# A convolution gate in front of a self-attention: the norm and pooling of the next image pair in pieces inside the attention loop

## The chip, the cores and the metric

The kernel runs on one core of one Trainium2 chip. The metric is the device time of one execution in microseconds (us). Five engines run their own instruction streams in order: PE (TensorE, matrix products), DVE (VectorE), ACT (ScalarE, which holds one set of function tables at a time), POOL (GpSimd) and SP (SyncE, which issues the DMAs here). Matrix products land in PSUM.

## The reference

A tensor `x` of 8 x 64 x 64 x 64 (images, channels C, rows, columns) goes through four layers: layer 0 is a selective scan followed by a gate (`_safm`), layer 1 a channel and a spatial self-attention, layer 2 a network with two inner training steps, layer 3 another spatial self-attention. The change touches the gate of layer 0 and the spatial attention of layer 1:

```
xo = (scan part of layer 0)
return xo + _safm(_channel_ln(xo, cn_g, cn_b), mfr_w, mfr_b, aggr_w, aggr_b)

def _channel_ln(x, g, b):                      # mean and variance over the channels
    return (x - u) * rsqrt(v + 1e-6) * g + b
def _safm(x, ...):                             # channels in 4 parts of 16
    for i in range(4):
        s = parts[i]; k = 2 ** i
        if i > 0: s = max-pool of s, k x k     # 32x32, 16x16, 8x8
        s = 3x3 depthwise convolution of s     # mfr_w[i]
        if i > 0: s = each value repeated k x k
    out = 1x1 convolution of all four parts + aggr_b
    return gelu(out) * x

# layer 1, per image; x is 64 channels x 4096 positions n
x1 = gamma_ca * (channel attention of x) + x
energy_s = q^T k                               # 4096 x 4096, q and k have 16 rows
out_s = v @ softmax(energy_s)^T
return x1 + gamma_sa * out_s + x
```

## The kernel before

`gate_and_attention` takes the images in four pairs; the two images of a pair lie on partitions 0 to 63 and 64 to 127, a row of 4096 positions each. For each pair `p` it does, in the order in which the code is written:

- **Load and norm.** `x` (2 MB, two buffers) is loaded. `Common.pair_norm` centres the channels with a matrix product (`cps`, L137: four tiles of 1024 positions, two products of 512 each), copies the centred values into the padded plane `pads[0]` (DVE, L140), squares them (ACT, L142) and averages the squares with a product that collects all eight blocks of 512 positions in one PSUM tile `var` of 16 rows (L145). Then come epsilon (DVE, L150), one square root (ACT, L151), one reciprocal (DVE, L152), and for each tile a product that spreads the 16 rows over the channels (`rps`, L157), a multiplication into the plane (DVE, L162) and gain and offset (ACT, L163).
- **Pooling.** Three levels of maxima over the whole plane, horizontally into `max1..3` (L1473) and vertically into `pads[1..3]` (L1475), on DVE.
- **Moves.** A convolution with 3 rows of taps is done as one product over 48 partitions per image (16 channels times 3 row offsets) for each of 3 column offsets. `move` (L1423) brings the three row offsets side by side: 6 DMAs from a plane to a tile `moved[i][r]` of 16 rows (32 rows of level 1 are two moves). A pair needs 8 moves, 48 DMAs, all issued by SP: four for level 0 in three rotating tiles, two for level 1, one each for levels 2 and 3.
- **The convolutions** (`conv`, L1433): levels 3, 2 and 1 (the root, whose results are doubled in size and added up by DVE), then four steps `j` of 1024 positions of level 0, each followed by an addition (DVE, L1454), GELU (ACT, L1504) and two POOL instructions (L1505, L1506) that put the result back into `x`.
- **Channel attention** (transposes and products, L1517 to L1543) and the projections `k` and `v` (`Attention.project`).
- **Spatial attention** (`Attention.run`): eight blocks `i` of 512 queries, each in 16 groups `g` of two key tiles `j`: four score products into two PSUM tiles `sc` (L1179; PSUM pool `sc` has three tiles of two banks, shared with `cps`, `rps` and the convolutions), two exponentials (ACT, L1184, into six rotating `ex` buffers), two additions to the running sum (DVE, L1191), and the products with `v` of the group before (L1198). At `g == 1` the next queries are projected, at `g == 3` `divide` sums and inverts (L1209 to L1219, a DVE reciprocal of 512 columns among it), at `g == 6` `finish` adds the channel mix (`fps`, L1548), writes `x2t` (L1550) and stores it. `qps`, `sumps` and `fps` share one PSUM bank of tag `mm`.

The order within each engine is not that of the code line by line: a planner at build time orders instructions by written priority, by when it reckons their inputs ready, and by free buffers, and adds the waits. Instructions that touch one PSUM bank from two engines are put one after the other. Layer 3 uses the same `Attention` class.

Of the kernel before, what the change touches and what calls it, by code (L numbers as in the profile page):

```python
# [10 lines left out]
F32 = mybir.dt.float32  # L11
BF16 = mybir.dt.bfloat16
AF = mybir.ActivationFunctionType
ALU = mybir.AluOpType
# [4 lines left out]
NB = 8  # L19
C = 64  # L20
S = 64
L = S * S
BK = 512
NBK = L // BK
# [20 lines left out]
class Common:  # L45
# [60 lines left out]
    def pair_norm_consts(self):  # L106

        nc = self.nc  # L110
        cen = self.tile([2 * C, 2 * C], "p_cen")
        nc.vector.memset(cen, 0.0)
        avg = self.tile([2 * C, 4 * NBK - 2], "p_avg")
        nc.vector.memset(avg, 0.0)
        for e in range(2):
            rows, m = slice(e * C, (e + 1) * C), 2 * NBK - 2 + e
            nc.vector.tensor_scalar(
                cen[rows, rows], self.ident[rows, rows], -1.0 / C, None, ALU.add
            )
            nc.vector.memset(avg[rows, m : m + 1], 1.0 / C)  # L120
        spread = self.tile([2 * NBK, 2 * NBK, C], "p_spread")
        nc.vector.tensor_copy(
            spread,
            self.ident[: 2 * NBK, : 2 * NBK].unsqueeze(2).to_broadcast([2 * NBK, 2 * NBK, C]),
        )
        return cen, avg, spread

    def pair_norm(self, work, sc, var, src, dst, consts, eps, g, b):

        nc = self.nc
        cen, avg, spread = consts
        for i in range(NBK // 2):
            ps = sc.tile([128, 2, BK], F32, name="cps", tag="sc")
            for e in range(2):
                nc.tensor.matmul(  # L137
                    ps[:, e, :], cen, src[:, bass.ts(2 * i + e, BK)], start=True, stop=True
                )
            nc.vector.tensor_copy(dst(i), ps.rearrange("p e (r c) -> p (e r) c", c=S))  # L140
            sq = work.tile([128, 2, BK], F32, name="sq", tag="blk", bufs=3)
            nc.scalar.activation(sq, ps, AF.Square)  # L142
            for e in range(2):
                m = 2 * (NBK - 1 - 2 * i - e)
                nc.tensor.matmul(  # L145
                    var[: 2 * NBK], avg[:, m : m + 2 * NBK], sq[:, e, :],
                    start=(i + e == 0), stop=(2 * i + e == NBK - 1),
                )
        rstd = work.tile([2 * NBK, BK], F32, name="rstd", tag="rstd", bufs=1)
        nc.vector.tensor_scalar(rstd, var[: 2 * NBK], eps, None, ALU.add)  # L150
        nc.scalar.activation(rstd, rstd, AF.Sqrt)  # L151
        nc.vector.reciprocal(rstd, rstd)  # L152
        for i in range(NBK // 2):
            ps = sc.tile([128, 2, BK], F32, name="rps", tag="sc")
            for e in range(2):
                j = 2 * (2 * i + e)
                nc.tensor.matmul(  # L157
                    ps[:, e, :], spread[:, j : j + 2, :].rearrange("k e c -> k (e c)"), rstd,
                    start=True, stop=True,
                )  # L160
            out = dst(i)
            nc.vector.tensor_tensor(out, out, ps.rearrange("p e (r c) -> p (e r) c", c=S), ALU.mult)  # L162
            nc.scalar.activation(out, out, AF.Identity, bias=b, scale=g)  # L163


class Background:
# [59 lines left out]
    def finish(self, b, count):  # L226

        while self.done.get(b, NBK) < count:
            self.credit = 1
            self.before(slots=NBK)  # L230
            self.after()
# [850 lines left out]
class Attention:  # L1082
# [74 lines left out]
        )  # L1157
        return k, v

    def run(self, p, x, k, v, finish):  # L1160


        cm, nc, d = self.cm, self.cm.nc, self.d
# [73 lines left out]
        for n in range(len(groups) + per):  # L1237
            now = []
            if n < len(groups):
                i, js = groups[n]  # L1240
                now = [(i, j, scores(i, j)) for j in js]
            for one in ahead:
                values(*one)
            ahead = now
            i, g = divmod(n, per)
            if g == 1 and i + 1 < NBK:
                queries(i + 1)
            if g == 3 and i > 0:
                done[i - 1] = divide(i - 1)
            if g == 6 and i > 0:  # L1250
                finish(i - 1, done.pop(i - 1))

    def out_of_range(self):

# [120 lines left out]
def gate_and_attention(cm, xh, w, a, x1, mixes, x2):  # L1375


    tc, nc = cm.tc, cm.nc
    halves = [slice(e * C, (e + 1) * C) for e in range(2)]
    with ExitStack() as ctx:  # L1380
        cm.open(ctx, "g_const")
        io = ctx.enter_context(tc.tile_pool(name="g_io", bufs=2))
        padp = ctx.enter_context(tc.tile_pool(name="g_pad", bufs=1))
        work = ctx.enter_context(tc.tile_pool(name="g_work", bufs=2))
        one = ctx.enter_context(tc.tile_pool(name="g_one", bufs=1))
        psum = ctx.enter_context(tc.tile_pool(name="g_psum", bufs=1, space=PSUM))
        sc = ctx.enter_context(tc.tile_pool(name="g_sc", bufs=3, space=PSUM))
        avp = ctx.enter_context(tc.tile_pool(name="g_av", bufs=1, space=PSUM))
        cn = cm.pair_norm_consts()
        cn_g, cn_b = cm.pair_column(w["cn_g"], "cn_g"), cm.pair_column(w["cn_b"], "cn_b")  # L1390
        fw, fb = safm_setup(cm, work, psum, w)
        att = Attention(
            cm, ctx, "sa", C // 4, a["wq"], a["bq"], a["wk"], a["bk"], a["wv"], a["bv"],
            a["gamma_sa"], work, psum, sc, avp,
        )
        gca = cm.tile([2 * C, 1], "gca")
        nc.sync.dma_start(gca, a["gamma_ca"].partition_broadcast(2 * C))
        pads = []
        for i in range(4):
            n = S // 2**i + 2  # L1400
# [4 lines left out]
        part = 16  # L1405
        moved = [
            [padp.tile([2 * C, min(part, S // 2**i), S // 2**i + 2], F32, name=f"mv{i}{r}",
                       tag=f"mv{i}{r}") for r in range(3 if i == 0 else 1 + (i == 1))]
# [7 lines left out]
        rows = BK // S  # L1416
        q = C // 4

        def move(i, r0, t):

            for e in range(2):
                for dy in range(3):
                    nc.sync.dma_start(  # L1423
                        t[e * C + dy * q : e * C + (dy + 1) * q],
                        pads[i][e * C + i * q : e * C + (i + 1) * q,
                                r0 + dy : r0 + dy + t.shape[1], :],
                    )
# [10 lines left out]
        def bank(n, cols):  # L1438
            ps = sc.tile([128, 2, BK], F32, name="cvps", tag="sc")
            return ps[:, 0, : n * cols].rearrange("p (r c) -> p r c", c=cols)  # L1440
# [10 lines left out]
        def add_doubled(dst, ps, d):  # L1451
# [5 lines left out]
                d.unsqueeze(2).to_broadcast([2 * C, n, 2, d.shape[2]]), ALU.add,  # L1457
            )

        for p in range(NB // 2):  # L1460
            x = io.tile([2 * C, L], F32, name="x", tag="x")
            nc.sync.dma_start(x, xh[2 * p : 2 * p + 2].rearrange("b c l -> (b c) l"))

            def inner(i):
                return pads[0][:, 1 + 2 * i * rows : 1 + 2 * (i + 1) * rows, 1 : S + 1]

            var = avp.tile([128, BK], F32, name="var", tag="av")
            cm.pair_norm(work, sc, var, x, inner, cn, 1e-6, cn_g, cn_b)
            src = pads[0][:, 1 : S + 1, 1 : S + 1]
            for i in range(1, 4):  # L1470
                n = S // 2**i
                m = one.tile([2 * C, 2 * n, n], F32, name=f"max{i}", tag=f"wide{n}")
                nc.vector.tensor_tensor(m, src[:, :, 0::2], src[:, :, 1::2], ALU.max)  # L1473
                src = pads[i][:, 1 : n + 1, 1 : n + 1]
                nc.vector.tensor_tensor(src, m[:, 0::2, :], m[:, 1::2, :], ALU.max)  # L1475
                for r, t in enumerate(moved[i]):
                    move(i, part * r, t)
            p3 = bank(8, 8)
            conv(p3, 3, moved[3][0], 0, 8)
            d3 = doubled(p3, 8, 8)  # L1480
# [11 lines left out]
            for j in range(NBK // 2):  # L1492
                blk = bass.ts(j, 2 * BK)
                t = moved[0][j % 3]
                move(0, 2 * j * rows, t)
                p0 = sc.tile([128, 2, BK], F32, name="cvps0", tag="sc")
                for e in range(2):
                    conv(p0[:, e, :].rearrange("p (r c) -> p r c", c=S), 0, t, e * rows, rows)
                t = work.tile([2 * C, 2 * rows, S], F32, name="gt", tag="blk", bufs=3)
                add_doubled(  # L1500
                    t, p0.rearrange("p e (r c) -> p (e r) c", c=S),
                    d1[:, j * rows : (j + 1) * rows, :],
                )
                nc.scalar.activation(t, t, AF.Gelu, bias=fb)  # L1504
                nc.gpsimd.tensor_tensor(t, t, inner(j), ALU.mult)  # L1505
                nc.gpsimd.tensor_tensor(  # L1506
                    x[:, blk], x[:, blk], t.rearrange("p r c -> p (r c)"), ALU.add
                )
# [5 lines left out]
            for j in range(TQ // 8):  # L1514
                ps = sc.tile([128, 8, 2 * C], F32, name="xTps", tag="sc")
# [37 lines left out]
                )  # L1553

            k, v = att.project(p, x)
            att.run(p, x, k, v, finish)
        bad, src = att.out_of_range(), att.src
    with tc.If(bad > 0):
        general_attention(cm, src, x1, mixes, x2)
# [634 lines left out]
```

## Time and profile before

| | us |
|---|---|
| three runs | 12187.44, 12193.51, 12204.01 |
| median | 12193.51 |
| profiled execution, its own time | 12199.93 |
| its span in the profile | 12198.2 |
| pair 0: first norm product to first convolution | 6961.76 to 7024.61 |
| attentions of the four pairs: first score product | 7083.17, 7599.60, 8114.06, 8630.54 |
| end of an attention's last sums to the next pair's first convolution | 7485.44 to 7542.05, 7998.71 to 8055.59, 8516.30 to 8573.13 |
| end of the last pair | 9036 |

The whole span is 12198.2 us: the scan layer until about 6950, the four pairs until about 9040, then layers 2 and 3. In a timeline row the columns are start, duration, engine, line and operation, output and input tiles, the number of instructions merged into the row, and in brackets the engine's idle time before it with what ended it. One 512-column fp32 product shows as two PE records. PEclk is the share of full clock that TensorE was granted. The PE end times are modelled.

### The profile page before, as it was taken

Reading aid. Unit: us, or ns where it says so; the run is one execution under the profiler, and the core shown is the slowest. Engines: PE = TensorE matmul, PEld = TensorE weight load, DVE = VectorE, ACT = ScalarE, POOL = GpSimd, SP = SyncE. Lnnn points to the kernel's source line nnn. Section 1 sums busy time; section 2 is a strip of 40 time slices with the busy share of each in tenths; the row PEclk is TensorE's granted clock in tenths of the full one; section 3 lists DMA queues with packets and bytes.
Section 4 is the critical chain, followed back from the end, with each engine's and each line's share of the span. In section 5 each row is a group of like instructions: output and inputs, shape, how many; then the busy total and the mean of one; then the engine's idle time right before and its main releaser. Section 6 shows DMA issues by size and latency. Waiting matters only on the chain. (4 is left out here: it accounts for less than half of the span.)

```text
span 12198.2 us, 120204 instructions
## 1 busy us (share of the span) xinstructions
PE 11171.0 (92%) x39087; PEld 4099.5 (34%) x39087; DVE 10381.2 (85%) x7400; ACT 7575.8 (62%) x10304; POOL 7249.5 (59%) x3326
## 2 busy tenths in 40 slices
PE   7899999999999999999998799999987779999999
PEld 2233333333333333333322233232335463333333
DVE  4999999999999999999999776868677686667767
ACT  4666667767667676676675554646547574555554
POOL 4999999999999999999999600000006490000000
PEclk8999999999999999999999899999998789999999
DMA  3666666666666666666666400000011100000000
GB/s 111 204 212 214 209 209 214 215 211 208 212 212 210 213 214 208 212 215 209 203 203 213 143 24 25 6 24 7 17 42 40 41 22 24 19 4 19 5 11 6
DMA packets 522900, 1528.64 MB, mean 125 GB/s; under 512 B 125312, under 2 KB 142352, under 8 KB 519696
## 3 DMA queue, kind: packets, MB, share of 16 engines
q1 hardware_dynamic: 522256, 1520.80, 37.9%
q8 instruction: 313, 5.13, 0.2%
q14 instruction: 331, 2.71, 0.1%
HBM read 1439.63 MB, written 72.09 MB: 124 GB/s over the span
## 5 line engine op out<-in xcount | busy, mean ns | idle before, releaser
L816 POOL TENSOR_TENSOR ct<-ct,h 128x1024 f32<-128x1024 f32 x2048 | 4796.4, 2369 | 297.0 <-DVE h L811 123.9
L882 PE MATMUL yps<-ct,lno_cen 128*128 128x512 f32 x8192 | 4119.2, 633 | 59.2 <-ACT yps L869 57.8
L811 DVE TENSOR_TENSOR_SCAN h<-a,state,z 128x1024 f32<-128x1024 f32 x1536 | 3571.0, 2341 | 84.0 <-ACT z L777 40.8
L762 ACT ACTIVATE a<-dt,amat 128x1024 f32<-128x1024 f32 x2048 | 2346.9, 1147 | 1136.5 <-DVE h L811 1132.3
L1191 DVE TENSOR_TENSOR sum<-sum,ex 128x1024 f32<-128x1024 f32 x1920 | 2347.9, 1223 | 633.0 <-ACT ex L1184 497.9
L1184 ACT ACTIVATE ex<-sc 128x1024 f32<-128x1024 f32 x2048 | 1968.1, 1024 | 1342.4 <-PE sc L1179 1342.0
L882 PEld LDWEIGHTS yps<-ct,lno_cen 128*128 128x128 f32 x8192 | 1475.9, 195 | 2077.1 <-issue 1810.5
L807 DVE TENSOR_TENSOR z<-z,e 128x1024 f32<-128x1024 f32 x1536 | 1860.0, 1211 | 125.2 <-PE z L780 77.7
L1198 PE MATMUL av<-ex,v 128*64 128x512 f32 x8192 | 1950.0, 604 | 0.0
L1179 PE MATMUL sc<-q,k 16*128 16x512 f32 (+1 forms) x8192 | 1562.2, 623 | 7.3 <-ACT q L1172 6.2
L780 PE MATMUL z<-bs,pick 48*128 48x512 bf16 x3072 | 940.6, 387 | 396.6 <-DVE h L811 348.4
L811 DVE TENSOR_TENSOR_SCAN h<-a,z 128x1024 f32<-128x1024 f32 x512 | 1162.0, 2281 | 81.3 <-ACT z L777 67.3
L770 POOL TENSOR_TENSOR bt<-bt,e 128x1024 f32<-128x1024 f32 x512 | 1212.9, 2369 | 5.2 <-PE cps L392 5.2
L1505 POOL TENSOR_TENSOR gt<-gt,pad 128x1024 f32<-128x1024 f32 x16 | 34.9, 2183 | 1574.3 <-ACT gt L1504 1574.3
L1198 PEld LDWEIGHTS av<-ex,v 128*64 128x64 f32 x8192 | 512.2, 136 | 1332.8 <-issue 1278.9
L1179 PEld LDWEIGHTS sc<-q,k 16*128 16x128 f32 (+1 forms) x8192 | 528.3, 184 | 1021.6 <-issue 976.6
L777 ACT COPY z<-bt 128x1024 f32<-128x1024 f32 x512 | 519.8, 1015 | 402.9 <-DVE h L811 302.9
L780 PEld LDWEIGHTS <-pick 48*128 48x128 bf16 x3072 | 175.4, 95 | 1515.4 <-DVE h L811 930.9
L534 PE MATMUL vps<-pad,convd 128*128 128x512 f32 x1152 | 574.8, 600 | 0.0
L1878 DVE RECIPROCAL r<-e 128x512 f32<-128x512 f32 x128 | 420.7, 3323 | 0.0
L1881 POOL TENSOR_TENSOR r<-r,half 128x512 f32<-128x512 f32 x128 | 162.7, 1271 | 366.7 <-issue 189.4
L798 ACT COPY state<-h 128x1 f32<-128x1 f32 x2048 | 363.1, 177 | 0.0
(417 smaller groups left out, 9581.1 us busy)
## 6 DMA issues: line engine op xcount, KB each, us to landing
ct<-bc SPq DMA_DIRECT2D x2048, 512.0 KB
bt<-bc SPq DMA_DIRECT2D x512, 512.0 KB
x<-x SPq DMA_DIRECT2D x12, 2048.0 KB
bc<-e SPq DMA_DIRECT2D x128, 128.0 KB
x<-x SPq DMA_DIRECT2D x32, 512.0 KB
part<-x SPq DMA_DIRECT2D x128, 128.0 KB
bsd<-bp SPq DMA_DIRECT2D x192, 64.0 KB
bs<-bsd SPq DMA_DIRECT2D x128, 96.0 KB
```

Of the source, the lines that this page charges most:

```text
L534: nc.tensor.matmul(held[0].rearrange("p (r c) -> p r c", c=S), convd[:, t, :], pad[:, j * rows + dy : (j + 1) * rows + dy, dx : dx + S], s ...
L762: ctl["exp", n] = nc.scalar.activation(ctl["a", n], ctl["dt"], AF.Exp, scale=amat[:, ctl["k"], n : n + 1])
L770: nc.gpsimd.tensor_tensor(bt, bt, ctl["dus"], ALU.mult)
L780: nc.tensor.matmul(z[:, bass.ts(i, BK)], pick[:, n : n + 1].to_broadcast([3 * N, DI]), ctl["bs"][:, bass.ts(i, BK)], start=True, stop=True,)
L807: first = nc.vector.tensor_tensor(z, z, ctl["dus"], ALU.mult)
L811: nc.vector.tensor_tensor_scan(h[:, flip], a[:, flip], z[:, flip], 0.0 if state is None else state[:, n : n + 1], ALU.mult, ALU.add,)
L816: freed[at] = nc.gpsimd.tensor_tensor(ct, ct, h, ALU.mult)
L882: nc.tensor.matmul(ctl["ps"][:, bass.ts(i, BK)], lno_cen, ct[:, bass.ts(i, BK)], start=False, stop=(n == N - 1 and not ctl["turns"]),)
L1179: nc.tensor.matmul(sc[:, e, :], k[r : r + d, bass.ts(j, 128)], qs[i][r : r + d, :], start=True, stop=True,)
L1184: nc.scalar.activation(ex, sc, AF.Exp)
L1191: nc.vector.tensor_tensor(sums[i], sums[i], ex, ALU.add)
L1198: nc.tensor.matmul(avs[i][r, :], v[:, j, r], ex[:, e, :], start=(j == 0), stop=(j == TQ - 1))
```

## The change

- `pair_norm` becomes a generator with `yield` after each half of the variance (two tiles, four blocks) and after each of the four output tiles. Each half has a `var` tile of 8 rows in the `mm` bank, its own square root (epsilon is now the activation's bias) and its own reciprocal, into a constant tile `p_rstd` at partitions 0 and 32; the spreading product now takes all 128 partitions. The square is written before the copy.
- Pooling is done per block of 16 rows in `ready(b)`, called after each output tile; the moves that a block makes possible follow at once, in an order written out.
- `normalize(p, own)` loads `x` and runs this generator. For pair 0 it runs to its end ahead of the loop, with `own` true: of each move's six DMAs SP issues three and ACT three. For pairs 1 to 3 it is handed to the attention of the pair before: `Attention.run` takes one step of it at `g == 10` of each block (load, two halves, four tiles: seven steps), and SP issues all.
- In the gate only the fourth move of level 0 is left (`j == 3`), divided between SP and ACT.

```diff
-    def pair_norm(self, work, sc, var, src, dst, consts, eps, g, b):
+    def pair_norm(self, work, sc, bank, src, dst, consts, g, b, ready):
...
-            nc.vector.tensor_copy(dst(i), ps.rearrange("p e (r c) -> p (e r) c", c=S))
             sq = work.tile([128, 2, BK], F32, name="sq", tag="blk", bufs=3)
             nc.scalar.activation(sq, ps, AF.Square)
+            nc.vector.tensor_copy(dst(i), ps.rearrange("p e (r c) -> p (e r) c", c=S))
+            h = i // 2
+            if i % 2 == 0:
+                var = bank("var")
             for e in range(2):
-                m = 2 * (NBK - 1 - 2 * i - e)
+                j = 2 * (i % 2) + e
+                m = 2 * (NBK - 1 - j)
                 nc.tensor.matmul(
-                    var[: 2 * NBK], avg[:, m : m + 2 * NBK], sq[:, e, :],
-                    start=(i + e == 0), stop=(2 * i + e == NBK - 1),
-                )
-        rstd = work.tile([2 * NBK, BK], F32, name="rstd", tag="rstd", bufs=1)
-        nc.vector.tensor_scalar(rstd, var[: 2 * NBK], eps, None, ALU.add)
-        nc.scalar.activation(rstd, rstd, AF.Sqrt)
-        nc.vector.reciprocal(rstd, rstd)
+                    var[:NBK], avg[:, m : m + NBK], sq[:, e, :], start=(j == 0), stop=(j == 3)
+                )
+            if i % 2:
+                mine = rstd[32 * h : 32 * h + NBK]
+                nc.scalar.activation(mine, var[:NBK], AF.Sqrt, bias=eps[:NBK])
+                nc.vector.reciprocal(mine, mine)
+                yield
...
             nc.scalar.activation(out, out, AF.Identity, bias=b, scale=g)
+            ready(i)
+            yield
...
+            if g == 10:
+                next(between, None)
...
-                    nc.sync.dma_start(
+                    (nc.sync, nc.scalar if own else nc.sync)[e].dma_start(
...
+            def ready(b):
+                src = pads[0][:, 1 + 16 * b : 17 + 16 * b, 1 : S + 1]
+                for i in range(1, 4):
+                    n, h = S // 2**i, 16 // 2**i
+                    m = maxima[i - 1][:, 2 * h * b : 2 * h * (b + 1), :]
+                    nc.vector.tensor_tensor(m, src[:, :, 0::2], src[:, :, 1::2], ALU.max)
+                    src = pads[i][:, 1 + h * b : 1 + h * (b + 1), 1 : n + 1]
+                    nc.vector.tensor_tensor(src, m[:, 0::2, :], m[:, 1::2, :], ALU.max)
+                if b:
+                    move(0, part * (b - 1), moved[0][b - 1], own)
+                if b == 2:
+                    move(1, 0, moved[1][0], own)
+                if b == 3:
+                    for i, r in ((3, 0), (2, 0), (1, 1)):
+                        move(i, part * r, moved[i][r], own)
...
+        for _ in normalize(0, True):
+            pass
         for p in range(NB // 2):
+            x = xs.pop(p)
...
-                move(0, 2 * j * rows, t)
+                if j == 3:
+                    move(0, 2 * j * rows, t, True)
...
-            att.run(p, x, k, v, finish)
+            following = normalize(p + 1, False) if p + 1 < NB // 2 else iter(())
+            att.run(p, x, k, v, finish, following)
+            for _ in following:
+                pass
```

More of the change, by code (lines that the diff above doesn't have):

```diff
@@ L120, in pair_norm_consts @@
             nc.vector.memset(avg[rows, m : m + 1], 1.0 / C)
[L121 to L124, printed above, removed]
-        )
-        return cen, avg, spread
-    def pair_norm(self, work, sc, var, src, dst, consts, eps, g, b):
+        spread = self.tile([128, 2 * NBK, C], "p_spread")
+        for h in range(2):
+            nc.vector.tensor_copy(
+                spread[:, h * NBK : (h + 1) * NBK, :],
+                self.ident[:, 32 * h : 32 * h + NBK].unsqueeze(2).to_broadcast([128, NBK, C]),
+            )
+        rstd = self.tile([128, BK], "p_rstd")
+        nc.vector.memset(rstd, 0.0)
+        eps = self.tile([128, 1], "p_eps")
+        nc.vector.memset(eps, 1e-6)
+        return cen, avg, spread, rstd, eps
+    def pair_norm(self, work, sc, bank, src, dst, consts, g, b, ready):
         nc = self.nc
-        cen, avg, spread = consts
+        cen, avg, spread, rstd, eps = consts
         for i in range(NBK // 2):
@@ L1158, in project, with run @@
         return k, v
-    def run(self, p, x, k, v, finish):
+    def run(self, p, x, k, v, finish, between=iter(())):
         cm, nc, d = self.cm, self.cm.nc, self.d
@@ L1417, in gate_and_attention, with move @@
         q = C // 4
-        def move(i, r0, t):
+        def move(i, r0, t, own):
             for e in range(2):
                 for dy in range(3):
-                    nc.sync.dma_start(
+                    (nc.sync, nc.scalar if own else nc.sync)[e].dma_start(
                         t[e * C + dy * q : e * C + (dy + 1) * q],
@@ L1458, in add_doubled, with inner @@
             )
-        for p in range(NB // 2):
[L1461 to L1477, printed above, removed]
+        def inner(i):
+            return pads[0][:, 1 + 2 * i * rows : 1 + 2 * (i + 1) * rows, 1 : S + 1]
@@ new lines, in gate_and_attention, with normalize @@
+        xs = {}
+        def normalize(p, own):
+            x = xs[p] = io.tile([2 * C, L], F32, name="x", tag="x")
+            nc.sync.dma_start(x, xh[2 * p : 2 * p + 2].rearrange("b c l -> (b c) l"))
+            yield
+            maxima = [
+                one.tile([2 * C, S // 2**i, S // 2 ** (i + 1)], F32, name=f"max{i}", tag=f"wide{S // 2 ** (i + 1)}")
+                for i in range(3)
+            ]
+            def ready(b):
[13 more added lines that the diff above has]
+                        move(i, part * r, moved[i][r], own)
+            yield from cm.pair_norm(
+                work, sc, lambda name: psum.tile([128, BK], F32, name=name, tag="mm"), x, inner,
+                cn, cn_g, cn_b, ready,
+            )
```

## The prediction

> **What bounds the kernel now.** The page comes first: one core, span 12198.2 us, and the four pairs of gate and attention in some 2080 us of it (6961.76 to 9036). Then the busy time by stretch: a gap between two attentions, the end of that gap, and one attention.
>
> ```profile
> core 0: us, PE busy (x) PEld busy (x) DVE busy (x) ACT busy (x) POOL busy (x), PEclk, DMA share, GB/s
> 7485.44:7542.05 56.61, 29.25 (x52) 9.82 (x51) 24.46 (x23) 10.97 (x10) 0.00 (x0) 0.67 0.21 59
> 7511.90:7542.05 30.15, 7.69 (x10) 2.50 (x9) 8.83 (x9) 3.73 (x3) 0.00 (x0) 0.50 0.18 32
> 7605.00:8005.00 400.00, 399.88 (x2099) 109.83 (x2099) 346.03 (x302) 254.32 (x268) 0.00 (x0) 1.00 0.02 5
> ```
>
> In the attention PE is busy 399.88 of 400 us at full clock; DVE has 54 us left, ACT 146. In the gap every engine is idle for half the time or more. The timeline of PE shows what the gap consists of:
>
> ```profile
> 7484.43 1.08 PE L1209 MATMUL sumps<-sum,all_ones 128*64 128x512 f32 x4
> 7485.44 4.56 PE L137 MATMUL cps<-x,p_cen 128*128 128x512 f32 x10
> 7489.83 1.02 PE L1548 MATMUL fps<-x,cmapT 128*128 128x512 f32 x2
> ...
> 7495.38 5.32 PE L145 MATMUL var<-sq,p_avg 128*16 128x512 f32 x12
> 7505.60 13.99 PE L157 MATMUL rps<-rstd,p_spread 16*128 16x512 f32 x16 [4.90 <-DVE rstd L152]
> 7542.05 29.87 PE L1433 MATMUL cvps<-mv,fw 128*128 128x64 f32 x72 [22.46 <-DMA mv<-pad]
> ```
>
> Norm, a wait for the root (4.90), `rps` at half speed (0.87 per record against 0.44 in `var`), then 22.46 us for the moves; after that the 72 convolution records run without a break. The table of waits and the rows of the DMA queue name the end of the gap:
>
> ```profile
> PE cvps L1433 <- DMA mv<-pad: 88.8, 4, 22.7
> ```
> ```profile
> L1423 SPq DMA_DIRECT2D mv<-pad x48: 507/587/935, 7511.9 to 7559.6; - x48
> ```
>
> SP needs 0.59 us for each issue, and 42 of the 48 stand ahead of the root, while the DMA engines are used to 0.18. Last, two groups of the attention:
>
> ```profile
> 7676.39 1.14 PE L1179 MATMUL sc<-q,k 16*128 16x512 f32 x8
> 7677.46 1.94 PE L1198 MATMUL av<-ex,v 128*64 128x512 f32 x8
> 7677.56 1.94 ACT L1184 ACTIVATE ex<-sc 128x1024 f32<-128x1024 f32 x2 [1.00 <-PE sc L1179]
> 7679.32 1.14 PE L1179 MATMUL sc<-q,k 16*128 16x512 f32 x8
> ```
>
> A group takes 2.94 us of PE; ACT waits 1.00 of it for scores. Whatever is put on PE here lengthens the attention by its full time; what is put on ACT or DVE does so only beyond their slack.
>
> **The change part by part.** The sum is made against the profiled execution: span 12198.2, 12199.93 with what lies around it. That is 6.4 us above the median of the three runs, so the difference is taken off 12193.5.
>
> *The three gaps go.* From the end of `sumps` to the first convolution: 56.61, 56.88 (7998.71 to 8055.59) and 56.83 us (8516.30 to 8573.13), together 170.3. What comes next on PE after the last sums is then the root, whose tiles landed blocks earlier: **-170.3**.
>
> *What stays of them.* `fps` of the last block lay inside the gap and now costs its two records, 0.86: **+2.6** for three. The root's products now meet the last `divide` on DVE (reciprocal 3.35, then 2.9 for `o`, the two range tests and `x2t`). PE has about 4.5 us of products (levels 3, 2, half of 1) before it needs the first doubling, which comes some 6 us after the sums: 1.5 us of waiting, at least 0, at most 8 if `divide` and root alternate on DVE: **+4.5**, ends 0 and 24. The rest of the gate is the same work, with the same end (POOL's last `x`, 7579.1).
>
> *PE work into the attention.* Per pair `cps` 16 records and `var` 16 at 0.43 (7485.97 to 7486.40 for consecutive loads), `rps` 16 at full clock instead of half, since the attention's clock is 1.00: 3 x 6.9 = 20.6. The projection of queries took 1.05 us for two records (7652.85 to 7653.90), so an insertion costs 0.19 besides; eight per pair (two in each half, one in each tile) make 1.5. Three pairs: **+66.4**. No cover is possible, PE being full.
>
> *DVE and ACT in the attention.* DVE per pair: four copies and four multiplications at 1.22, two reciprocals of 3.34 (8 rows take as long as 16: the same 512 columns; one more than before), pooling of about 2.0 per block by the rows of its smaller levels (0.69, 0.43, 0.29, 0.23 and two of 0.2), together 24.6 against 54 of slack. ACT: squares 1.02, offsets 1.24, two roots of 0.63, and four table loads of 1.28 where one stood (to Sqrt and back to Exp, twice): 15.5 against 146. Both fit on average, so what counts is the moment. A half puts 1.28 + 0.63 + 1.28 between exponentials, and behind the waiting Sqrt all later exponentials queue; PE has 0.9 us in hand before the `v` products run dry (the exponentials end at 3.1 into the group, the products start at 4.0), but also the 6.9 us of norm records of the half to run meanwhile. A tile takes one of three `sc` tiles until DVE has read it; with two left, scores wait for the exponentials, 0.2 us per group. Lower end 0, as the planner can fill each wait with score groups. Upper end: per half twice the longest wait of `var` for a square (1.5) plus 3.2 minus 0.9, 5.3; per tile four groups of 0.3, 1.2; 15.4 per pair. I take 1.5 per half and 0.5 per tile, near the lower end, because in the nearest rows (the `divide` insertions with 6 us of DVE work) PE goes on unbroken: **+15**, ends 0 and 46. If this cover failed, the moved ACT and DVE work would show in full, 40 us per pair.
>
> The trace has table loads of 1283 ns. The Trainium skill, "ScalarE: Activation LUTs", section "Table sets: the hidden batching unit", asks to do all exps together, then all sqrts, and puts a switch at about 2.7 us; that speaks against this change. By its figure twelve loads on the path would be an estimate of 32 us in place of my 15, and the sum would be -69.
>
> *Moves.* For pairs 1 to 3 the 42 issues (25 us of SP) spread over five blocks of 50 us; behind them on SP stand only the `x2t` stores, whose buffer is needed 50 us later, and the next load of `x`, needed a block later: nothing. The fourth move waits for the convolution of step 0 as before, now with three issues on each queue. On ACT they stand ahead of the first GELU: 3 x 0.59 = 1.8, of which 1.3 falls into ACT's wait for the addition (L1454, 1.23). POOL's chain starts with that GELU and ends the gate, so 0.5 to 1.8 per pair: **+4**, ends 2 and 7.
>
> *Pair 0.* From the first norm product to the root: 6961.76 to 7024.61. The last offset ends at 7004.55, limited by loads of weights (DVE has `rps` ready at 6985 and multiplies at 6992), which also cover the second reciprocal of 3.3. One block's pooling ends near 7006.6, nine issues (the last three moves) of 0.59 on each queue near 7012, landing near 7015: 10 gained, less 2 for offsets that now queue behind issues on ACT: **-8**, ends 0 and -14. The Trainium skill, "DMA: Bandwidth & Descriptors", section "Issuing engines are not separate DMA queues", says that a second issuer saves only sequencer time, usually small beside the DMA. By that this term would be near 0 and the sum -78; the DMA share of 0.18 during the wait speaks for the issue as the limit here.
>
> Sum: -170.3 + 2.6 + 4.5 + 66.4 + 15 + 4 - 8 = **-86**, so 12108. All lower ends: -115; all upper ends: -24.
>
> **The rivals.**
>
> *The attention is held up more (R1).* Sqrt waiting for `var` in ACT's order, or `var` for its square, costs 3 us at each of the 18 pieces (two halves and four tiles, three times), 54 instead of 15: -47, 12147. For it: `var` did wait for squares ten times in the gaps (8.2 us). Against: there the order was copy first. The skill's rule on table sets points this way.
>
> *The pieces do not come where they are written (R2).* The planner sets the order: in the rows above `cps`, written after `fps`, runs ahead of it. If it lets the pieces slide to the end of the attention, the gap keeps its 57 us and only small terms change: 12190, within 15. Against: the pieces carry an earlier written priority than the later groups, and `qps` and `sumps` come out where they are written.
>
> *Slower: each piece stops PE (R3).* One mechanism: a `cps` or `rps` tile keeps its `sc` tile until DVE comes to it, DVE is behind by its `divide` and the new reciprocals, scores lack a tile, so exponentials and then `v` products stand. Without stalls the change gains 101, so it decides from 101 / 18 = 5.6 us per piece. At 8 us (DVE's `divide` of 6.3 plus a multiplication) it gives 144 - 101 = +43, 12237. For it: DVE is at 346 of 400 and needs some 30 us of a block to catch up after a `divide`. Against: at `g == 10` most of that is caught up, and each piece itself gives DVE PE time in which no new exponentials come.
>
> **How the numbers follow.** A measurement of this kernel can tell about 0.2%, 24 us, from no change. Forecast 0.62 (its own range 12078 to 12140), R1 0.20, R2 0.08, R3 0.10. Faster: forecast and R1, 0.82; same: R2; slower: R3. The range runs from all lower ends (12078) to all upper ends (12170), with R1 inside.
>
> **What would show it.** Right: first convolutions of pairs 1 to 3 follow the last `sumps` within 3 us, no wait of `cvps` for `mv` beyond 1 us there, attentions of about 428 instead of 401 us (pairs 0 to 2), the fourth as before, `rps` at 0.43 per record, nine more table loads, pair 0's first convolution about 8 us earlier. Wrong: waits of `sc` or `av` for ACT or DVE of tens of us per attention (R1, R3), or `cps` rows behind the last `sumps` (R2). I would be most wrong about the order within the halves, which no row of the profile before shows.

## The result, and the profile after

| | before | after |
|---|---|---|
| median of five runs each, taken side by side (us) | 12193.51 | 12130.14 |
| lowest and highest | 12187.44, 12210.48 | 12125.25, 12137.26 |
| ratio after / before | | 0.9946, 95% interval 0.9931 to 0.9960 |
| profiled execution, its span | 12198.2 | 12123.5 |

The change makes the kernel 63.4 us faster, about 0.5%, and the interval of the ratio leaves out 1. The direction is as forecast and the time inside the range, but the gain is 22 us less than the forecast of 86. Of the 74.7 us between the two spans 9.3 lie ahead of the first norm product (6961.76 before, 6952.42 after), in the scan layer, which the change does not touch; in the other kernels run here that product starts anywhere from 6949.8 to 6966.7. So the comparison is made from the first norm product to the last `fps`: 2071.43 us before, 2007.77 after, **63.7 less**, which agrees with the medians. All tables below use this stretch.

The busy time by stretch, first for the convolutions that now follow an attention, then for the attention of pair 0 (first scores to the start of the last sums), then for a stretch of 400 us inside the next attention:

```profile
core 0: us, PE busy (x) PEld busy (x) DVE busy (x) ACT busy (x) POOL busy (x), PEclk, DMA share, GB/s
7523.47:7552.00 28.53, 28.53 (x76) 13.58 (x75) 12.98 (x16) 4.73 (x4) 11.27 (x6) 1.00 0.31 98
7089.81:7522.46 432.65, 431.18 (x2153) 118.36 (x2153) 367.47 (x332) 271.30 (x285) 0.00 (x0) 0.98 0.04 9
7600.00:8000.00 400.00, 398.91 (x2026) 109.70 (x2018) 344.17 (x317) 254.90 (x267) 0.00 (x0) 1.00 0.04 10
```

PE is nearly as full as before (398.91 of 400), but the attention is 31 us longer and its clock is 0.98 on average: somewhere it was not 1.00. The convolutions run at full clock without a break. PE's timeline at the place where the gap was:

```profile
7522.46 1.08 PE L1220 MATMUL sumps<-sum,all_ones 128*64 128x512 f32 x4
7523.47 4.81 PE L1446 MATMUL cvps<-mv,fw 128*128 128x64 f32 x18
7528.11 1.02 PE L1585 MATMUL fps<-x,cmapT 128*128 128x512 f32 x2
7528.97 23.34 PE L1446 MATMUL cvps<-mv,fw 128*128 128x512 f32 x54
```

The first convolution starts 1.01 us after the last sums start, in all three places; in the table below the gap counts as 0. `fps` slips in between the levels, and the 54 larger records follow with no bracket, so without a wait. In the table of waits, `cvps` on `mv` had 88.8 us in four waits before; now two of these remain, both in pair 0, and two waits of pair 0 are new in the list:

```profile
ACT sq L146 <- PE var L154: 34.3, 1, 34.3
...
PE bps L1088 <- DMA mb<-in_L_conv_mfr_b_dram: 21.8, 1, 21.8
...
PE cvps L1446 <- DMA mv<-pad: 15.7, 2, 13.1
```

Stage by stage (us, pairs 0 to 3):

| | before | after | difference | forecast |
|---|---|---|---|---|
| pair 0, first norm product to first convolution | 62.85 | 75.66 | **+12.8** | -8 |
| gaps after the last sums, three | 56.61, 56.88, 56.83 | 0, 0, 0 | **-170.3** | -170.3 |
| first convolution to first score | 58.56, 57.55, 58.47, 57.41 | 61.73, 56.51, 56.51, 56.51 | **-0.7** | +11.1 |
| first score to the start of the last sums | 401.26, 398.10, 401.23, 398.11 | 432.65, 427.78, 431.46, 401.39 | **+94.6** | +81.4 |
| sum | | | **-63.6** | -85.8 |

Of the -0.7 in the third row, pairs 1 to 3 are -3.9 and pair 0 is +3.2; pair 0 waits a second time for a move there (2.6 us, the rest of the 15.7 in the table of waits).

What the attention pays can be read off single pieces. A half of the norm, PE and ACT:

```profile
7175.76 3.70 PE L142 MATMUL cps<-x,p_cen 128*128 128x512 f32 x8
...
7179.40 3.60 PE L154 MATMUL var<-sq,p_avg 128*8 128x512 f32 x8
...
7180.60 1.28 ACT L159 ACT_TABLE_LOAD   x1
7182.93 1.14 PE L1190 MATMUL sc<-q,k 16*128 16x512 f32 x8
7183.03 0.68 ACT L159 ACTIVATE p_rstd<-var,p_eps 8x512 f32<-8x512 f32 x1 [1.15 <-PE var L154]
7183.73 1.28 ACT L1195 ACT_TABLE_LOAD   x1
7184.00 1.94 PE L1209 MATMUL av<-ex,v 128*64 128x512 f32 x8
7185.02 3.95 ACT L1195 ACTIVATE ex<-sc 128x1024 f32<-128x1024 f32 x4
7185.86 1.36 PE L1190 MATMUL sc<-q,k 16*128 16x512 f32 x8
```

The norm's 16 records hold PE from 7175.76 to the scores at 7182.93, 7.16 us. Both table loads, the root and a wait fall beside PE's work; all that shows of them is that the second group of scores takes 1.36 instead of 1.14. A half costs 7.16 + 0.22 = 7.38 us. An output tile, all engines but the weight loads:

```profile
7290.50 1.98 PE L166 MATMUL rps<-p_rstd,p_spread 128*128 128x512 f32 x4
7292.41 1.14 PE L1190 MATMUL sc<-q,k 16*128 16x512 f32 x8
7293.30 1.22 DVE L171 TENSOR_TENSOR pad<-pad,rps 128x1024 f32<-128x1024 f32 x1
7293.48 1.94 PE L1209 MATMUL av<-ex,v 128*64 128x512 f32 x8
7294.55 1.24 ACT L172 ACTIVATE pad<-pad,cn_b,cn_g 128x1024 f32<-128x1024 f32 x1 [3.88 <-DVE pad L171]
7295.35 1.13 PE L1190 MATMUL sc<-q,k 16*128 16x512 f32 x4
7295.70 3.74 ACT L1195 ACTIVATE ex<-sc 128x1024 f32<-128x1024 f32 x4
...
7296.75 1.13 PE L1190 MATMUL sc<-q,k 16*128 16x512 f32 x4 [0.27 <-ACT ex L1195]
```

Here something does show. The offset (L172) waits 3.88 us for DVE's multiplication, at the head of ACT's queue. The scores of 7292.41 end by 7293.55, but their exponentials start only at 7295.70, behind the offset. So the next score products come in two parts, 4 records and 4 records, and each part takes as long (1.13) as all 8 together (1.14). That and a pause of 0.27 make 1.39: a tile costs 1.91 + 1.39 = 3.30 us. All six halves and all twelve tiles show these costs. Together they are 83.9 of the 94.6; the rest is PE at half clock, as in the first `v` products after one of the splits, which take 3.24 instead of 1.94, and in the window around them:

```profile
7351.09 3.24 PE L1209 MATMUL av<-ex,v 128*64 128x512 f32 x8
```
```profile
7351.00:7355.00 4.00, 4.00 (x14) 1.18 (x16) 3.83 (x8) 1.72 (x2) 0.00 (x0) 0.57 0.55 91
```

In pair 0, PE's timeline from the norm products to the first convolution:

```profile
6956.07 5.42 PE L142 MATMUL cps<-x,p_cen 128*128 128x512 f32 x12
6983.34 0.38 PE L1088 MATMUL bps<-mb,aggr 64*64 64x1 f32 x4 [21.85 <-DMA mb<-in_L_conv_mfr_b_dram]
...
6991.45 6.14 PE L154 MATMUL var<-sq,p_avg 128*8 128x512 f32 x8 [0.31 <-DVE sa_wv L87]
...
7028.08 1.51 PE L1446 MATMUL cvps<-mv,fw 128*128 128x64 f32 x6 [13.14 <-DMA mv<-pad]
```

`cps` ends at 6961.5; `var` should follow its squares, but comes 30 us later, behind set-up products that wait for small loads.

### The profile page after: what moved, and what is told of

Same layout as the page of the kernel before. It is cut to its first block, busy times and chain, and to the rows that moved or that the text cites. A ratio compares the mean times of both kernels' runs of the same rounds, so it can differ in the third digit from the quotient of the medians.

```text
span 12123.5 us, 120280 instructions
## 1 busy us (share of the span) xinstructions
PE 11166.1 (92%) x39087; PEld 4089.4 (34%) x39087; DVE 10396.8 (86%) x7475; ACT 7588.3 (63%) x10317; POOL 7249.7 (60%) x3326
## 5 line engine op out<-in xcount | busy, mean ns | idle before, releaser
L1190 PE MATMUL sc<-q,k 16*128 16x512 f32 (+1 forms) x8192 | 1577.7, 624 | 11.1 <-ACT q L1183 6.2
L822 DVE TENSOR_TENSOR_SCAN h<-a,z 128x1024 f32<-128x1024 f32 x512 | 1161.5, 2281 | 76.1 <-ACT z L788 61.1
```

The costliest lines, as they stand in the source:

```text
L822: nc.vector.tensor_tensor_scan(h[:, flip], a[:, flip], z[:, flip], 0.0 if state is None else state[:, n : n + 1], ALU.mult, ALU.add,)
L1190: nc.tensor.matmul(sc[:, e, :], k[r : r + d, bass.ts(j, 128)], qs[i][r : r + d, :], start=True, stop=True,)
```

## The experiments

Theory A: pair 0 is late because `var` now shares the single `mm` bank with the set-up products, which wait for loads of weights. For the tiles of the attention there were two theories. C: the offset stands in ACT's queue ahead of the exponentials. D: the `sc` tile that `rps` holds until DVE has read it is what the scores lack (the mechanism of R3). Each time is the median of its runs; the medians of the kernel before in the same jobs were 12192.68 (the first four), 12191.51 (the next three) and 12193.12 (the last).

**Pair 0: its own bank (e1).** The change, but `var` of pair 0 comes from the bank of tag `av` as before the change:

```diff
-   work, sc, lambda name: psum.tile([128, BK], F32, name=name, tag="mm"), x, inner,
+   work, sc, lambda name: (avp.tile([128, BK], F32, name=name, tag="av") if own
+                           else psum.tile([128, BK], F32, name=name, tag="mm")), x, inner,
```

> The changed kernel, but for pair 0 alone the two var tiles lie in the bank of tag av, which is free then, instead of the mm bank that the set-up products (tps, bps) use. Theory A (in pair 0 the norm queues behind the set-up's loads of weights, because both need the one mm bank): from the first norm product to the first convolution 55 us (48 to 63) instead of 75.7, pairs 1 to 3 unchanged, time 12130 - 20 = 12110 (12100 to 12118). Rival B (pair 0 is late from the second root and from the moves that stand in ACT's order): the stretch stays within 3 us of 75.7 and the time within 5 us of 12130.

12101.29 us (12096.00 to 12121.91), ratio 0.9932 (0.9919 to 0.9946). Pair 0 takes 52.43 us instead of 75.66; PE's timeline:

```profile
6953.90 1.98 PE L142 MATMUL cps<-x,p_cen 128*128 128x512 f32 x4
6955.81 3.60 PE L154 MATMUL var<-sq,p_avg 128*8 128x512 f32 x8
...
6981.06 0.28 PE L1088 MATMUL bps<-mb,aggr 64*64 64x1 f32 x4 [1.56 <-DMA mb<-in_L_conv_mfr_b_dram]
...
7002.56 1.51 PE L1446 MATMUL cvps<-mv,fw 128*128 128x64 f32 x6 [13.28 <-DMA mv<-pad]
```

`var` runs among the `cps` products, and `bps` waits 1.56 instead of 21.85 us with nothing behind it. The shared bank cost 23.2 us. Against before, pair 0 is now 10.4 us shorter: the forecast of -8 (0 to -14) would have fitted a kernel with this bank. The rest of the region is within 3 us of the kernel after; all experiments below start from e1.

**The divided moves (e2).** e1 with all moves on SP:

```diff
-   (nc.sync, nc.scalar if own else nc.sync)[e].dma_start(
+   nc.sync.dma_start(
```

> As e1, but SP issues all moves (no ACT issues, neither in pair 0 nor for the fourth move of level 0). If the issue time of one queue is the limit: pair 0's first convolution 6 us later than in e1 (3 to 12), the gates of pairs 1 to 3 within 1 us, since ACT's three issues fall into a wait: about +6 against e1. Rival (a second issuer saves next to nothing): within 1 us of e1 in pair 0.

12110.71 us (12103.75 to 12120.81). The times of e1 and e2 overlap, so the comparison rests on the stage in one trace of each: pair 0 takes 59.00, 6.6 more than e1. SP's queue shows why, first e2, then e1:

```profile
6992.91 26.94 SPq L1436 DMA_DIRECT2D mv<-pad  x42
```
```profile
6989.53 16.39 SPq L1436 DMA_DIRECT2D mv<-pad  x21
```

The same 42 transfers keep SP busy for 26.9 us alone and for 16.4 us if ACT issues half. From first convolution to first score pairs 1 to 3 take 56.5 us in both, so dividing the fourth move there neither costs nor gains. The rule of the Trainium skill cited in the prediction ("DMA: Bandwidth & Descriptors", section "Issuing engines are not separate DMA queues": a second issuer saves only sequencer time, usually small beside the DMA) is right in that issue time is what was saved; for these 42 moves it was not small, 6.6 of 59.0 us.

**The table switches (e3).** e1 with the root left out: its activation is Identity, which needs no table load (the trace has 13 fewer than that of e1), so the inverse of the variance takes the place of the inverse root.

```diff
-   nc.scalar.activation(mine, var[:NBK], AF.Sqrt, bias=eps[:NBK])
+   nc.scalar.activation(mine, var[:NBK], AF.Identity, bias=eps[:NBK])
```

> As e1, but the square root is left out of the norm (the function is Identity), so that the output is another one; no table load stands between the exponentials any more, all else is the same. If the switches are hidden behind the PE records of the half: a half costs the attention 7.2 us as against 7.4 in the changed kernel, the three attentions together 1 to 3 us less. Rival (the switch of tables is on the path): 2.6 us per half, 15 us less in all.

One run, 12113.06 us. PE around a half:

```profile
7161.76 3.70 PE L142 MATMUL cps<-x,p_cen 128*128 128x512 f32 x8
7165.39 3.60 PE L154 MATMUL var<-sq,p_avg 128*8 128x512 f32 x8
7168.92 1.14 PE L1190 MATMUL sc<-q,k 16*128 16x512 f32 x8
7169.99 1.94 PE L1209 MATMUL av<-ex,v 128*64 128x512 f32 x8
7171.86 1.14 PE L1190 MATMUL sc<-q,k 16*128 16x512 f32 x8
```

Now the second scores take 1.14 as well. Two switches are worth 0.22 us per half, the same in all six, 1.3 in the whole kernel. The time of the run and the attentions (425.60, 427.32, 434.20) can't show so little: by the half-clock stretches they scatter more.

**The pieces after the attention (e4).** e1, with the generator run to its end behind each attention instead of inside it:

```diff
-   att.run(p, x, k, v, finish, following)
+   att.run(p, x, k, v, finish)
```

> As e1, but the norm, pooling and moves of pairs 1 to 3 come after the attention of the pair before instead of inside it (two roots, pooling per block and the order of the moves stay as changed, SP issues all). If the move into the attention brings the gain: the attentions last 401 us again, the three gaps come back with 45 to 55 us each, 84 less in the attentions and 150 more in the gaps, so about +66 against e1 (45 to 85), 12176. Rival (most of the gain is the order of the moves and the pooling per block): gaps of 25 to 35, within 15 of e1.

12161.61 us, ratio 0.9972 (0.9961 to 0.9983): 60.3 slower than e1 by the medians, 61.1 by the region. PE behind an attention:

```profile
7476.12 1.08 PE L1220 MATMUL sumps<-sum,all_ones 128*64 128x512 f32 x4
7477.12 4.56 PE L142 MATMUL cps<-x,p_cen 128*128 128x512 f32 x10
...
7524.60 1.51 PE L1446 MATMUL cvps<-mv,fw 128*128 128x64 f32 x6 [18.00 <-DMA mv<-pad]
```

The gaps are back (47.47, 46.55, 47.59) and the attentions are at 398 to 401 again. So the halves, the pooling per block and the order of the moves gain 9 to 10 us per gap by themselves, but some 3 of these are lost up to the first scores (60.4 to 61.4 us against 57.4 to 58.5). With pair 0 (52.74 us, its bank given back), all parts but the place come to 28.7 us of region against before; the place of the pieces is worth 61.

**The tiles later in the block (e5).** e1 with the pieces put four groups further from `divide`:

```diff
-            if g == 10:
+            if g == 13:
```

> As e1, but the pieces come at g == 13 of each block instead of g == 10. In the changed kernel a tile's piece costs the attention 3.30 us: 1.91 for the rps records, 1.39 after it, where the second pair of scores runs by itself. There DVE was 0.8 us behind when rps was done, and ACT stood 3.88 us in front of the offset. If DVE's backlog after divide decides the 1.39, it is 0.7 or less here (12 tiles, 8 us less, 12093); if not, it stays at 1.39 and the time within 3 us of e1.

12079.01 us, ratio 0.9909 (0.9893 to 0.9926). A tile pays 0.62 instead of 1.39 beyond its records, a half 0.22 as before, and attentions 0 to 2 take 423.27, 423.04 and 426.34. DVE is less behind here and multiplies 2.0 us after the first `rps` record instead of 2.8:

```profile
7268.42 1.98 PE L166 MATMUL rps<-p_rstd,p_spread 128*128 128x512 f32 x4
...
7270.44 1.22 DVE L171 TENSOR_TENSOR pad<-pad,rps 128x1024 f32<-128x1024 f32 x1
...
7271.70 1.25 ACT L172 ACTIVATE pad<-pad,cn_b,cn_g 128x1024 f32<-128x1024 f32 x1 [3.11 <-DVE pad L171]
```

The offset waits 3.11 instead of 3.88 us, 0.77 less, and a tile pays 0.77 less. Both C and D expect that; the next two separate them. The three attentions are 20 us shorter than in e1: 9 for the twelve tiles, near the 8 expected, and 11 because fewer half-clock stretches fell into them.

**The offset off ACT (e6, e7).** e1 with gain and offset of pairs 1 to 3 as one instruction of POOL (e6) or of DVE (e7):

```diff
-            nc.scalar.activation(out, out, AF.Identity, bias=b, scale=g)
+            if own:
+                nc.scalar.activation(out, out, AF.Identity, bias=b, scale=g)
+            else:
+                nc.gpsimd.tensor_scalar(out, out, g, b, ALU.mult, ALU.add)   # e7: nc.vector
```

> As e1, but for pairs 1 to 3 gain and offset of the norm are done by POOL, which is idle in the attention, instead of ACT. Theory C (the offset waits in ACT's order for DVE's multiplication and holds up the exponentials behind it): the 1.39 after a tile's rps go, a tile costs 1.9 to 2.1, the half-clock stretches after them go too, the three attentions are 15 to 25 us shorter together, about 12082. Rival D (the rps tile holds one of three sc tiles until DVE has read it): a tile still costs 3.2 to 3.4 and the time stays within 4 us of e1.

> As e6, but DVE does gain and offset right behind its multiplication. Theory C: a tile costs 1.9 to 2.3 as in e6 (DVE has 1.2 us more per tile, within its slack), 12082 to 12088. Rival D: 3.2 to 3.4 as in e1.

e6: 12069.49 us, ratio 0.9899 (0.9882 to 0.9915). e7: 12063.97, 0.9899 (0.9883 to 0.9916). In both, attentions 0 to 2 take 420.53 to 420.59. A tile of e7:

```profile
7262.68 1.98 PE L166 MATMUL rps<-p_rstd,p_spread 128*128 128x512 f32 x4
7264.59 1.14 PE L1193 MATMUL sc<-q,k 16*128 16x512 f32 x8
7265.47 1.22 DVE L171 TENSOR_TENSOR pad<-pad,rps 128x1024 f32<-128x1024 f32 x1
...
7265.77 1.94 ACT L1198 ACTIVATE ex<-sc 128x1024 f32<-128x1024 f32 x2 [2.92 <-PE sc L1193]
7266.73 0.81 DVE L175 TENSOR_SCALAR pad<-pad,cn_g,cn_b 128x1024 f32<-128x1024 f32 x1
7267.53 1.14 PE L1193 MATMUL sc<-q,k 16*128 16x512 f32 x8
```

DVE comes to `rps` as late as in the kernel after (2.8 us after its first record), yet the exponentials start 1.2 us after their scores do, against 3.3, and the next 8 score records stay together. Each of the twelve tiles costs its 1.91 us and nothing more, so D falls and C is shown. An attention is 398.1 + 2 x 7.38 + 4 x 1.91 = 420.5: no half-clock stretch is left in these three. Together they are 31 us shorter than in e1, more than the 15 to 25 expected: 12 x 1.39 = 16.7 for the tiles, the rest for the half-clock stretches. e6 and e7 cannot be told apart. Both are faster than before, e7 by 128 us, and than the kernel after, e7 by 66 us (that one was timed in another job, whose kernel before was 2 us slower).

**The set-up loads (e8).** e7 with the 24 loads of `ftaps`, which stand on SP ahead of the moves of pair 0, issued by ACT:

```diff
-   nc.sync.dma_start(taps[r, i, :], w["mfr_w"][i][:, dy, :])
+   nc.scalar.dma_start(taps[r, i, :], w["mfr_w"][i][:, dy, :])
```

> As e7, but the 24 loads of the convolution taps at set-up are issued by ACT instead of SP, whose issues stood until 6989 in front of pair 0's first moves in e1. If SP's issue queue still bounds pair 0: from the first norm product to the first convolution 44 us (40 to 48) instead of 51.9, pairs 1 to 3 as in e7, 8 us less than e7. Rival (pair 0 is bound by the chain of norm, pooling and moves by now, or ACT's issues delay the squares): within 3 us of 51.9.

12064.14 us, as e7. Pair 0 takes 53.47 instead of 51.85: the rival holds, not the 44 expected. ACT's timeline says why:

```profile
6957.27 12.41 ACTq L1075 DMA_DIRECT2D ftaps<-in_L_conv_mfr_w_dram  x24
...
6969.78 1.94 ACT L146 ACTIVATE sq<-cps 128x1024 f32<-128x1024 f32 x2 [19.50 <-DMA ftaps<-in_L_conv_mfr_w_dram]
```

The issues stand in ACT's own order ahead of the first square, which starts right behind them. It comes 11.3 us after the first norm product instead of 3.9 in e7, so the norm starts 7.4 us later, about as much as SP is relieved (its set-up loads end 30.8 instead of 38.9 us after that product).

## Why the prediction was right or wrong

- **What bounds, and the gaps: right.** -170.3 forecast and measured, and nothing took the gaps' place. R2 (pieces sliding to the end) did not happen; e4 shows what it would have looked like.
- **"What stays of them" and the fourth move: too high by about 12.** +11.1 forecast, -0.7 measured (-3.9 in pairs 1 to 3, +3.2 in pair 0). The products of the levels and `fps` cover `divide`, the convolutions run at clock 1.00 without the gap ahead of them, and the fourth move on two queues costs nothing that e2 could find.
- **"PE work into the attention": right.** 7.16 us per half and 1.91 per tile are 65.9 for three pairs, 66.4 forecast.
- **"DVE and ACT in the attention": the total nearly right, its parts wrong.** Forecast 1.5 per half and 0.5 per tile, +15. Measured 0.22 per half and 1.39 per tile: 6 x 0.22 + 12 x 1.39 = 18.0. That the totals agree is luck: the halves were put too high by 7.7 and the tiles too low by 10.7. The table loads, over which the prediction worried, lie beside the norm's own records (e3). What the working of the tile overlooked is the order on ACT: it looked at who keeps the `sc` tile, not at what stands behind the waiting offset. By the table-set rule of the Trainium skill ("ScalarE: Activation LUTs", section "Table sets: the hidden batching unit") the twelve loads, on the path, would have been an estimate of 32 us; e3 puts them at 1.3.
- **The clock in the attention: a missing term, about 10.7.** The prediction took 1.00 throughout. Of this 3.3 lies in the fourth attention, which has no pieces; stretches of that size also stood at the start of two attentions before (401.26 and 401.23 against 398.1; the granted clock is 0.66 over 7083.17 to 7093.17 and 1.00 over the first 10 us of the next attention), and the prediction took its 1.00 from the attention between these two, which has none.
- **"Pair 0": the step that failed.** -8 forecast, +12.8 measured. The working followed loads, DVE and the two DMA queues, but not the bank from which the new `var` tiles come: the diff takes pair 0's `var` from a bank of its own into the shared `mm`. e1 gives the bank back and gets -10.4, of which e2 shows 6.6 to come from dividing the moves; that fits the rest of the working. This one step is 20.8 us, nearly all of the 22 that were missing, because the other two errors, -11.8 in the gate and +13.2 in the attention, happen to cancel: that is luck too.
- **R1 and R3.** Nothing like 3 us or more was lost per piece: 18.0 over 18 pieces is 1.0 on average. R3's mechanism is refuted for the tiles by e7, where the `sc` tile is held as long and nothing is lost; a half loses no more than 0.22.
- **Slips in the working.** PE was busy 29.25 of the 56.61 us of a gap, a little more than half. Of the ten waits of `var` for a square that R1 counts, only six (4.6 of the 8.2 us) lie in the three gaps, the rest in pair 0. The lower ends add up to -113, not -115. None of this changes the forecast.

## What to carry to other kernels

When work is put into a loop that one engine fills, price it by that engine's records, and then go through each instruction that waits on another in-order engine: what is queued behind it is held up for its wait and its own length together. Here 1.24 us of offset on ACT, behind a wait of 3.88, cost 1.39 of PE per tile, and as 0.81 us on DVE, which had slack and does the step before it anyway, nothing. When code is made to serve two places, look up which buffer each of its tiles now comes from in each place; a single-buffered PSUM tag shared with set-up work cost 23 us, more than a tenth of what the three gaps gave.

## What the runs showed of the hardware

- A group of eight score records on 16 rows takes 1.14 us when it is issued together, and four of them issued alone take 1.13: splitting the group costs a full 1.13 us, not a half.
- The granted clock fell to 0.57 over 7351 to 7355 (0.50 over 7353 to 7355) although PE had been busy for 10.73 of the 11 us before, with one pause of 0.27. "TensorE: Matmul & The Clock Gate" of the Trainium skill, section "Part 1: The HAM clock gate (the "warmup" mystery)", ties the slow clock in its table of states to an idle window of about 3.4 us; the length of the stretch fits that figure (the 0.43 missing over 4 us are 1.7 us, which 3.4 us at half clock would give), the idle time does not. Around the tiles these stretches came only after split scores, at four of the twelve tiles of the kernel after, and are gone without them (e6, e7). What sets them off, there and at the start of some attentions, stays open.
- 24 small loads took 12.41 us to issue on ACT (0.52 each), as long as twelve exponentials of 1.02; an issue is not free for the engine that makes it.
